# Segmented attention with batch norm: the start in another order, on other engines

## The chip, the cores and the metric

The kernel runs on one core of a Trainium2 chip. The metric is device time of one launch in microseconds (us), the median of several runs. The core has five engines with queues of their own: TensorE (PE, whose weight loads show as PEld), VectorE (DVE), ScalarE (ACT), GpSimd (POOL) and SyncE (SP). Each works through its own instructions in order and waits on semaphores for the others. SP, ACT and POOL also issue DMA transfers.

## The reference

16384 rows of 256 numbers belong to 8 segments by an id for each row (`bids`, here not sorted). Attention runs inside each segment, over at most 3072 positions.

```python
def _L0_rec_ref(feat, bids, Wq, Wk, Wv, Wt, gamma, beta):
    B = 8; LMAX = 3072; EPS = 1e-05; NEG = -1000000000.0
    N, d = feat.shape
    q = feat @ Wq
    k = feat @ Wk
    v = feat @ Wv
    starts = jnp.searchsorted(bids, jnp.arange(B, dtype=bids.dtype))
    pos = jnp.arange(N, dtype=bids.dtype) - starts[bids]
    def pad(x):
        return jnp.zeros((B, LMAX, x.shape[-1]), x.dtype).at[bids, pos].set(x)
    qp, kp, vp = (pad(q), pad(k), pad(v))
    mask = jnp.zeros((B, LMAX), bool).at[bids, pos].set(True)
    scores = jnp.einsum('bld,bmd->blm', qp, kp)
    scores = jnp.where(mask[:, None, :], scores, NEG)
    attn = jax.nn.softmax(scores, axis=-1)
    rp = jnp.einsum('blm,bmd->bld', attn, vp)
    r = rp[bids, pos]
    t = r @ Wt
    mu = t.mean(axis=0)
    var = t.var(axis=0)
    tn = (t - mu) / jnp.sqrt(var + EPS) * gamma + beta
    return feat + jax.nn.relu(tn)
```

Since the ids are not sorted, `starts` is the result of a binary search on unsorted data, and a row owns its slot only if its position falls inside the segment's window and no later row writes the same slot. So each segment has a few hundred owners, whose rows have to be found and gathered.

## The kernel before

All of it is written by hand in `fast_path`: the order of the calls of `pg` is the order of each engine's instructions, and `Program.op` works out which semaphores an instruction waits for from the places that it reads and writes (a strided write counts as the whole stretch between its first and last element). Only where a segment holds more than 4 tiles of 128 owners do the instructions for tiles 4 and 5 run (`present`, `given`: a branch on the tile count in `tiles_i`, which each engine loads into a register).

**The start (lines 1070 to 1425).** SP loads the ids (`b_i`), ACT the weights: `wv_sb`, `wt_sb`, and `w4`, which holds Wq three times and Wk once. SP also fills the rows' buffer `xs` of all 8 segments with zeros by eight DMAs (`zero_fill`), since a gather leaves a row alone where the index is out of range. DVE sets constants. Then comes the first list: segment 0's owners have a mask (`own0`); `scan` counts them along a partition into `lm`; `prefix` lets PE sum over the partitions (`tri`, `onesb`) and DVE derive where each partition's owners begin and end (`cbeg`, `cend`, `n_bc`, `tiles_i`); `list_tests` compares slot numbers with these (`ge`); `list_half` multiplies `lm` and `ge` on PE for three tiles, and its `finish` counts on DVE (`lr`, `junk`, `jc`) the index of each slot's row (`idx`) and lets POOL issue three gathers. Ten DVE instructions (`nwi` to `sm`) build a matrix for the binary search, which then runs in three steps of small products and comparisons (`less`, `hit1`, `hit2`, `stv`) to the starts `st_bc`. With them `owners(e)` finds the owners of any segment (6 operations and a scan), here of segment 1, whose list follows. PE then multiplies Wv and Wt (`wvT`, `wvt`), DVE sets six PSUM banks to 1.0, and segment 0's rows are transposed (`xT`, less the first tile's mean `negx`) and projected (`project`: q and k, from q and k copies of PSUM), give values (`values`, into `vs`, whose last column is ones for the softmax's sum) and scores with their exponentials (`scores`, `pa`). Banks for these come from `nb()`, which hands out two in turn.

**The segments (lines 1642 to 1700).** For segment e and tile u: `attend` multiplies exponentials and values, `attended` takes the reciprocal (`rdens`) on DVE and scales on ACT (`tk`), and in fixed steps u the next segment is transposed, projected and scored, the list of segment e + 2 is made, and column sums go on (`moments`, `acc`). Between them `slot(n)` takes n pieces of other work from a queue, by the table `plan_of`: first `everyone()` (a, b, c, d: positions and owners of all rows; f: the scans of segments 3 to 7 and of the losers; g: their prefix and the list tests of segment 3; h: how often each slot is read; g2: a table of output groups), then `tables()` and `one_hot()`.

**The end.** Rows outside the first six segments' slots are looked up again (`others`), the batch norm's sums are closed, and all groups of rows get their result added and stored.

## Time and profile before

| what | value |
|---|---|
| median of 3 runs | 338.47 us (337.35 to 339.0) |
| the profiled execution | 340.09 us |
| its span, first to last instruction | 337.7 us |
| PE, DVE, ACT, POOL busy in the span | 253.6, 231.1, 128.9, 130.9 us |
| mean granted TensorE clock | 0.882 |
| chain that ended last, by engine | PE 50%, DVE 19%, DMA 11%, issue 9%, POOL 6%, ACT 3% |
| first gather of rows, POOL | at 10.04 us |
| first product of exponentials and values, PE | at 49.76 us |

The profile comes from one execution and gives each instruction's start and duration, what its engine waited for, and the chain of work that ended last, followed back from the last instruction. A row of the timeline reads: start in us, duration in us, engine, line of the kernel (often that of a helper, so the tile's name says more), operation, what it writes and reads, its shape, how many were merged, and in brackets how long the engine had stood idle and who released it. PE's spans are modelled at their ends, so a busy PE need not be a fast one; the granted clock is shown apart.

### The profile page before, as it was taken

The numbers are of one execution on the slowest core, as the hardware profiler recorded it, in microseconds if no ns is written. First come the engines' busy times: TensorE is split into PE (matmuls) and PEld (weight loads), VectorE is DVE, ScalarE is ACT, GpSimd is POOL, SyncE is SP. The second block draws the span as 40 slices with busy tenths as digits, with TensorE's granted clock in tenths as the row PEclk, the third lists the DMA queues.
The fourth block names the chain that finished last, engine by engine and source line by source line (L and its number), as shares of the span: only waits on it lengthen the run. The fifth ranks groups of instructions, "written<-read, shape, count | busy, mean of one in ns | idle before, by whom it ended". The sixth has DMA issues, their size and how long they took to land.

```text
span 337.7 us, 4437 instructions
## 1 busy us (share of the span) xinstructions
PE 253.6 (75%) x1192; PEld 170.3 (50%) x1192; DVE 231.1 (68%) x714; ACT 128.9 (38%) x281; POOL 130.9 (39%) x143
## 2 busy tenths in 40 slices
PE   2227679689799989999999999939729889755100
PEld 1225347477487677777878778627513323112000
DVE  6677437966989898636665676737389999995400
ACT  0011343426756648644755664544402323121100
POOL 2617004306034015005721760741021146887775
PEclk9999698969899999999999999996957989895755
DMA  7992001213112103203030321592998899999982
GB/s 238 339 319 65 2 0 33 79 52 97 63 61 66 64 32 88 66 3 117 19 104 32 84 86 56 174 333 53 325 423 355 296 423 418 423 394 416 415 325 83
DMA packets 26186, 59.27 MB, mean 176 GB/s; under 512 B 5408, under 2 KB 18802, under 8 KB 22058
## 3 DMA queue, kind: packets, MB, share of 16 engines
q1 hardware_dynamic: 19242, 48.06, 38.6%
q0 software_dynamic: 5280, 10.18, 9.4%
q10 hardware_dynamic: 1632, 0.66, 0.7%
q8 instruction: 14, 0.23, 0.3%
q14 instruction: 18, 0.15, 0.2%
HBM read 26.80 MB, written 28.74 MB: 164 GB/s over the span
## 4 chain that ended last, share of the span: by engine, by line
PE 50%; DVE 19%; DMA 11%; issue 9%; POOL 6%; ACT 3%; POOLq 1%; DVEq 0%; ACTq 0%; SPq 0%
PE ps L807 47%; DMA out<-f 8%; POOL out L892 5%; PE ps L812 3%; DVE f L826 2%; DMA tl<-t_rows,ridl 2%; DVE tk L826 2%; ACT pa L817 1%; DVE acc L846 1%; DVE junk L833 1%; DVE w L826 1%; DVE k L823 1%; POOL xl L882 1%; DMA b_i<-in_r_bids 1%; DVE lm L855 1%
## 5 line engine op out<-in xcount | busy, mean ns | idle before, releaser
L882 POOL DMA_INDIRECT xs<-in_r_feat,idx x48 | 50.5, 1053 | 129.6 <-DVE idx L846 68.7
L807 PE MATMUL ps<-vs,pa 128*128 128x257 f32 x312 | 77.9, 403 | 6.5 <-ACT vs L822 4.6
L807 PEld LDWEIGHTS ps<-vs,pa 128*128 128x128 f32 x312 | 61.0, 201 | 18.5 <-ACT vs L822 5.0
L892 POOL DMA_INDIRECT out<-tk,idx x39 | 45.7, 1171 | 30.7 <-DVE f L826 14.6
L807 PE MATMUL ps<-wvt,xT 128*128 128x256 f32 x156 | 42.3, 424 | 1.7 <-DVE own L835 1.6
L817 ACT ACTIVATE tk<-ps,rdens 128x256 f32<-128x256 f32 x46 | 22.2, 482 | 55.7 <-DVE rdens L859 55.6
L807 PE MATMUL ps<-f,ident 128*128 128x512 f32 x56 | 35.0, 755 | 6.1 <-DMA f<-in_r_feat 6.1
L807 PEld LDWEIGHTS ps<-wvt,xT 128*128 128x128 f32 x156 | 32.2, 212 | 13.1 <-issue 3.2
L822 ACT COPY f<-ps 128x512 f32<-128x512 f32 x28 | 15.0, 589 | 54.8 <-PE ps L807 54.8
L807 PE MATMUL ps<-y,hot 48*128 48x256 bf16 x128 | 16.4, 312 | 14.7 <-DVE f L826 8.1
L817 ACT ACTIVATE pa<-ps,mask 128x512 f32<-128x512 f32 x39 | 23.9, 691 | 7.2 <-PE ps L807 7.2
L826 DVE TENSOR_TENSOR f<-f,ps 128x512 f32<-128x512 f32 x36 | 22.3, 681 | 4.2 <-DMA f<-in_r_feat 3.4
L826 DVE TENSOR_TENSOR tk<-tk,ss 128x1024 f32<-128x1024 f32 (+1 forms) x30 | 24.3, 848 | 0.3
L846 DVE SCALAR_TENSOR_TENSOR acc<-sq,reads_r,acc 128x256 f32<-128x256 f32 x45 | 21.6, 479 | 4.1 <-ACT sq L817 4.0
L823 DVE COPY k<-ps 32x128 f32<-32x128 f32 x40 | 11.8, 294 | 17.0 <-PE ps L807 16.2
L807 PEld LDWEIGHTS ps<-y,hot 48*128 48x128 bf16 x128 | 5.5, 101 | 35.0 <-issue 13.5
L846 DVE SCALAR_TENSOR_TENSOR acc<-tk,reads_r,acc 128x256 f32<-128x256 f32 x45 | 21.4, 476 | 1.2 <-ACT tk L817 0.6
L807 PEld LDWEIGHTS ps<-f,ident 128*128 128x128 f32 x56 | 11.2, 227 | 19.3 <-issue 10.7
L807 PE MATMUL ps<-q,k 32*128 32x512 f32 (+2 forms) x154 | 18.7, 478 | 2.9 <-ACT pa L817 2.9
L807 PE MATMUL ps<-xT,w 128*128 128x512 f32 (+1 forms) x60 | 20.1, 468 | 0.2 <-ACT xT L817 0.2
L807 PE MATMUL ps<-vs,pb 128*128 128x257 f32 x82 | 19.6, 388 | 0.0
L807 PEld LDWEIGHTS ps<-vs,pb 128*128 128x128 f32 x82 | 15.1, 190 | 6.5 <-issue 2.3
(249 smaller groups left out, 353.0 us busy)
## 6 DMA issues: line engine op xcount, KB each, us to landing
f<-in_r_feat SPq DMA_DIRECT2D x16, 1024.0 KB, 13.8
out<-f SPq DMA_DIRECT2D x16, 1024.0 KB, 11.7
xs<-zt SPq DMA_DIRECT2D x8, 768.0 KB, 10.8
t_rows<-tk SPq DMA_DIRECT2D x8, 512.0 KB, 2.9
t_rows<-tk SPq DMA_DIRECT2D x8, 256.0 KB, 2.3
eb<-edge_of SPq DMA_DIRECT2D x16, 96.0 KB, 2.4
xs<-in_r_feat,idx POOLq DMA_INDIRECT x48, 2.8
out<-tk,idx POOLq DMA_INDIRECT x39, 6.6
```

The lines of the kernel that those rows point to most:

```text
L807: "PE", lambda e: e.matmul(out, lhsT, rhs, start=start, stop=stop, skip_group_check=True),
L812: return self.op("PE", lambda e: e.transpose(out, in_, ident), [in_, ident], [out])
L817: "ACT", lambda e: e.activation(out, in_, func, bias=bias, scale=scale), [in_, *more], [out]
L822: return self.op("ACT", lambda e: e.copy(out, in_), [in_], [out])
L823: return self.op(eng, lambda e: e.tensor_copy(out, in_), [in_], [out])
L826: return self.op(eng, lambda e: e.tensor_tensor(out, a, b, op), [a, b], [out])
L833: lambda e: e.tensor_scalar(out, a, s1, s2, op0, op1, accum_out=accum)
L846: else e.scalar_tensor_tensor(out, a, s, b, op0, op1),
L855: "DVE", lambda e: e.tensor_tensor_scan(out, a, b, 0.0, ALU.mult, ALU.add), [a, b], [out]
L882: lambda e: e.indirect_dma_start(out=out, out_offset=None, in_=table, in_offset=bass.IndirectOffsetOnAxis(ap=ind, axis=0), bounds_check=n ...
L892: lambda e: e.indirect_dma_start(out=table, out_offset=bass.IndirectOffsetOnAxis(ap=ind, axis=0), in_=src, in_offset=None, bounds_check=n ...
```

## The change

The order of the start is written anew, and some work changes its engine.

- Constants: the ten instructions `nwi` to `sm` stand ahead of the ids' cast. `zt` and several constants are set by POOL. Later, DVE's memsets of `vs`'s ones, `acc`, `xl`, `tl`, `ridl` and `ecat` go to POOL too, behind the gathers of segment 1.
- Loads: Wq and Wk are loaded once each, on SP's queue behind the ids; ACT makes the two further copies of Wq.
- Zeros and blanks: ACT writes the zeros of `xs` for segments 0 to 2 and the ones of the six banks. The DMA fills of segments 3 to 7 stay on SP's queue, behind the small loads.
- First list: `prefix` returns three parts (`first`, `then`, `last_`) that are called apart, `list_tests` has two parts, and the search's products and comparisons stand between those of the list.
- Value weights: PE turns and multiplies them between the search's steps.
- Segment 0: each tile is transposed on its own (`turned`), in two banks, and moved in two halves.
- Segment 3 gets `owners` of its own as one piece of work (`third`), after b; the scans and the prefix of `everyone` begin at segment 4, and `steps` says in which steps a piece is taken.

On ACT, this stood from the start to the first activation that writes `xT` before:

```order
L877 DMA wv_sb<-in_L_rec_Wv 128x2x256
L877 DMA wt_sb<-in_L_rec_Wt 128x2x256
L877 DMA w_68<-in_L_rec_Wq 128x2x32
L877 DMA w_68<-in_L_rec_Wq 128x2x32 [waits of_ACT_2]
L877 DMA w_68<-in_L_rec_Wq 128x2x32 [waits of_ACT_3]
L877 DMA w_68<-in_L_rec_Wk 128x2x32 [waits of_ACT_4]
L694 BRANCH_PREFETCH_HINT
L688 TENSOR_LOAD tiles_i [waits at_DVE]
L688 ISA x2
L822 ACT_TABLE_LOAD
L822 COPY wvT<-ps 128x256 [waits at_PE] x2
L822 COPY wvt<-ps 128x256 [waits at_PE] x2
```

And this stands there now (`w_68` is `w4`, `of_SP_2` the landing of Wk):

```order
L822 ACT_TABLE_LOAD
L822 COPY ps<-ones 128x512 [waits at_DVE]
L822 COPY ps<-ones 128x512
L822 COPY xs<-zt 128x1536 [waits at_POOL]
L822 COPY ps<-ones 128x512 x4
L822 COPY w_68<-w_68 128x2x32 [waits of_SP_2]
L822 COPY w_68<-w_68 128x2x32 [waits at_ACT]
L822 COPY xs<-zt 128x1536
L822 COPY wvT<-ps 128x256 [waits at_PE] x2
L822 COPY wvt<-ps 128x256 [waits at_PE]
L822 COPY xs<-zt 128x1536
L822 COPY wvt<-ps 128x256 [waits at_PE]
```

The blanks, zeros and copies of Wq are new there, ahead of the value weights' copies; the register load moved behind `xT`.

POOL's queue from its constants on (each DMA row is one gather of 128 rows; the twelve are segment 0's and segment 1's) is changed thus:

```order
 L694 BRANCH_PREFETCH_HINT
+L865 MEMSET reads_r 128x48
+L865 MEMSET eps_t 128x1
+L865 MEMSET ones_n 128x128
+L865 MEMSET rdens 128x48
+L865 MEMSET graw 128x64
 L882 DMA xs<-in_r_feat,idx 128x256 x12
+L865 MEMSET vs_61 128x6
+L865 MEMSET vs_66 128x6
+L865 MEMSET acc 128x512
+L865 MEMSET xl 128x768
+L865 MEMSET tl 128x768
```

The memsets of `vs_61` (`vs[0]`, segment 0's values) stand behind all twelve gathers; ACT's first copy into it waits for POOL.

On PE, in segment 0's steps (the first piece is behind tile 3's product, the second stood ahead of segment 1's second values), the prefix of the fourth list moves up and gets one column:

```order
@@ -99,4 +104,6 @@
 L772 UNCONDITIONAL_BRANCH
 L807 MATMUL ps<-vs_61,pa_60 128x257
+L807 MATMUL ps<-lm,tri 128x1
+L807 MATMUL ps<-lm,onesb 128x1
 L772 COMPARE_AND_BRANCH
 L807 MATMUL ps<-xT,w_68 128x128 x2
@@ -125,6 +132,4 @@
 L807 MATMUL ps<-vs_61,pb 128x257 x6
 L772 UNCONDITIONAL_BRANCH
-L807 MATMUL ps<-lm,tri 128x6
-L807 MATMUL ps<-lm,onesb 128x6
 L807 MATMUL ps<-wvt,xT 128x256 x4
```

The prefix of segments 4 to 7 and of the losers, now five columns, is taken in segment 1. The diff, cut to its core:

```diff
+    pg.dma("SP", w4[:, :, 0:DQ], wq.rearrange("(h p) m -> p h m", p=P))
+    pg.dma("SP", w4[:, :, 3 * DQ : 4 * DQ], wk.rearrange("(h p) m -> p h m", p=P))
...
-    zero_fill(0)
+    blank(slice(4, 6))
+    zero_rows(0)
+    blank(slice(0, 4))
+    for g in (1, 2):
+        pg.copy("ACT", w4[:, :, g * DQ : (g + 1) * DQ], w4[:, :, 0:DQ])
+    zero_rows(1)
...
+    sA, sB = ps_o
+    pg.mm(sA[:, 0:NB], sm[:], less[:])
+    pg.mm(sB[:, 256:257], sm[:], ones[:, 0:1])
+    first()
+    list_tests(0, FT, 0)
+    h0 = list_half(0, 0, nb())
+    then()
...
+    pg.mm(sB[:, 0:NB], b_f[:], hit1[:])
+    h1 = list_half(0, 1, nb())
+    list_tests(0, FT, 1)
+    h0()
...
+    pg.mm(sA[:, 0:NB], sm[:], less[:])
+    wv_turned(0)
+    wv_turned(1)
+    h1()
...
+    wv_wt(0)
+    pg.mm(sB[:, 0:NB], ones[:], stv[:])
...
+    zero_rows(2)
...
+    bx = [bank[0], bank[1]]
+    def turned(t):
+        for h in range(DH):
+            pg.tr(bx[h][:, t * P : (t + 1) * P], xs[:, t, h * P : (h + 1) * P], ident[:])
+    last_()
+    owners(1)
+    turned(0)
+    for h in range(DH):
+        pg.red(xsum[:, h : h + 1], bx[h][:, 0:P])
+    wv_wt(1)
+    turned(1)
+    first, then, last_ = prefix(1, 2)
...
+    first()
+    list_tests(1, FT, 0)
+    turned(2)
...
+        into_xT(h, 0, QB, bx[h][:, 0:QB])
+    h0, h1 = list_half(1, 0, ps_s[2]), list_half(1, 1, ps_s[3])
+    turned(3)
...
+        into_xT(h, QB, QA, bx[h][:, QB:QA])
+    h0()
     for eng in ("PE", "ACT", "DVE"):
         pg.register(eng, 0, tiles_i[0:1, 0:1], 2)
...
     project(0, 0)
     xt_rest(0)
+    h1()
+    last_()
+    for i in range(2):
+        pg.set("POOL", vs[i][:, :, D : D + 1], 1.0)
+    pg.set("POOL", acc[:], 0.0)
...
+    for e in range(3, NB):
+        pg.dma("SP", xs[:, e * FT : (e + 1) * FT, :], zt[:].unsqueeze(1).to_broadcast([P, FT, D]))
     values(0, 0)
...
-            for e in range(3, NB):
+            for e in range(4, NB):
                 pg.scan(lm[:, e, 0:J], ones[:], o3[:, e, :])
...
-    plan_of = {(0, u): n for u, n in enumerate((0, 1, 2, 1, 1, 1))}
-    for e in range(1, NB - 1):
-        for u in range(FT):
-            plan_of[(e, u)] = 1 if e > 3 else int(u in ((0, 2, 4) if e == 1 else (0, 2, 3, 5)))
-    work.extend(everyone())
+    steps = {0: (1, 2, 3, 4, 5), 1: (0, 1, 2, 4, 5), 2: (0, 2, 3, 5), 3: (0, 1, 2, 3, 5)}
+    def third():
+        owners(3)
+        first, then, last_ = prefix(3, 4, ps_s[3])
+        first()
+        then()
+        last_()
+        list_tests(3, FT)
+    todo = everyone()
+    work.extend([*todo[0:2], third, *todo[2:]])
```

More of the change, by code (lines that the diff above doesn't have):

```diff
@@ L1097, in fast_path @@
-    pg.set("DVE", eps_t[:], EPS)
-    pg.set("DVE", ones_n[:], 1.0 / N)
-    pg.set("DVE", rdens[:], 1.0)
+    pg.ts(nwi[:, 0:1], pci[:], -1, ALU.mult)
+    pg.tt(nwi[:, 0:1], nwi[:, 0:1], pci[:], ALU.bitwise_and)
+    pg.copy("DVE", wfl[:, 0:1], nwi[:, 0:1])
+    pg.tt(wfl[:, 1:2], pcol[:], wfl[:, 0:1], ALU.subtract)
+    pg.tt(wfl[:, 0:1], pcol[:], wfl[:, 0:1], ALU.add)
+    pg.ts(sa[:], irow[:], pcol[:], ALU.is_ge)
+    pg.stt(sm[:], irow[:], wfl[:, 0:1], sa[:], ALU.is_lt, ALU.mult)
+    pg.ts(sc_[:], irow[:], wfl[:, 1:2], ALU.is_ge)
@@ L1107, in fast_path @@
+    blank(slice(4, 6))
[4 more added lines that the diff above has]
+    zero_rows(1)
     pg.dma("SP", bs_i[0 : P - PS, :], bids2[PS:P, :])
     pg.dma("SP", br_i[PS:P, :], bids2[0 : P - PS, :])
-    for e in range(1, NB):
-        zero_fill(e)
-    pg.set("DVE", graw[:], 0.0)
+    pg.set("POOL", reads_r[:], 0.0)
+    pg.set("POOL", eps_t[:], EPS)
+    pg.set("POOL", ones_n[:], 1.0 / N)
+    pg.set("POOL", rdens[:], 1.0)
@@ L1112, in fast_path @@
+    pg.set("POOL", graw[:], 0.0)
     for i in range(4):
@@ new lines, in fast_path, with wv_turned, wv_wt @@
+    pg.ts(hit1[:], sA[:, 0:NB], popc[:, 0:1], ALU.is_equal)
+    pg.mm(sB[:, 0:NB], b_f[:], hit1[:])
+    h1 = list_half(0, 1, nb())
+    list_tests(0, FT, 1)
+    h0()
+    pg.tt(less[:], sB[:, 0:NB], ecol[:], ALU.is_lt)
+    pg.ts(ident[:], irow[:], pcol[:], ALU.is_equal)
+    def wv_turned(m):
+        b = bank[m]
+        for h in range(DH):
+            pg.tr(b[:, h * P : (h + 1) * P], wv_sb[:, h, m * P : (m + 1) * P], ident[:])
+        pg.copy("ACT", wvT[:, m, :], b[:, 0:D])
+    def wv_wt(h):
+        b = bank[2 + h]
+        for m in range(DH):
+            pg.mm(b[:, 0:D], wvT[:, m, h * P : (h + 1) * P], wt_sb[:, m, :], start=(m == 0), stop=(m == 1))
+        pg.copy("ACT", wvt[:, h, :], b[:, 0:D])
@@ L1358, in fast_path @@
     pg.tt(stv[:], stv[:], lowp[:], ALU.add)
-    ps = nb()
-    pg.mm(ps[:, 0:NB], ones[:], stv[:])
-    pg.copy("DVE", st_bc[:], ps[:, 0:NB])
+    wv_wt(0)
+    pg.mm(sB[:, 0:NB], ones[:], stv[:])
+    pg.copy("DVE", bs_f[:], bs_i[:])
+    pg.tt(same[:], bs_f[:], b_f[:], ALU.is_equal)
+    pg.copy("DVE", st_bc[:], sB[:, 0:NB])
     pg.ts(st_lo[:], st_bc[:], -float(LMAX), ALU.add)
     pg.ts(st_hi[:], st_bc[:], float(LMAX), ALU.add)
-    pg.copy("DVE", bs_f[:], bs_i[:])
-    pg.tt(same[:], bs_f[:], b_f[:], ALU.is_equal)
+    zero_rows(2)
     def owners(e):
@@ L1379, in fast_path @@
+    h0()
     for eng in ("PE", "ACT", "DVE"):
         pg.register(eng, 0, tiles_i[0:1, 0:1], 2)
-    for m in range(DH):
-        b = nb()
-        for h in range(DH):
-            pg.tr(b[:, h * P : (h + 1) * P], wv_sb[:, h, m * P : (m + 1) * P], ident[:])
-        pg.copy("ACT", wvT[:, m, :], b[:, 0:D])
-    for h in range(DH):
-        b = nb()
-        for m in range(DH):
-            pg.mm(b[:, 0:D], wvT[:, m, h * P : (h + 1) * P], wt_sb[:, m, :], start=(m == 0), stop=(m == 1))
-        pg.copy("ACT", wvt[:, h, :], b[:, 0:D])
@@ L1393, in fast_path @@
-    pg.tr32(gb[:].rearrange("p s i -> p (s i)"), graw[:].rearrange("p s i -> p (s i)"))
-    for b in bank[0:6]:
-        pg.set("DVE", b[:], 1.0)
-    for i in range(2):
-        pg.set("DVE", vs[i][:, :, D : D + 1], 1.0)
-    pg.set("DVE", acc[:], 0.0)
-    pg.ts(rc[:], n_bc[:, 0:1], float(P), ALU.min, 1.0, ALU.max)
-    pg.recip(rc[:], rc[:])
-    bx = [nb(), nb()]
-    for t in range(4):
-        for h in range(DH):
-            pg.tr(bx[h][:, t * P : (t + 1) * P], xs[:, t, h * P : (h + 1) * P], ident[:])
@@ L1425, in fast_path @@
     owners(2)
-    list_tests(2, FT)
+    first, then, last_ = prefix(2, 3)
+    first()
+    list_tests(2, FT, 0)
+    then()
+    list_tests(2, FT, 1)
+    last_()
+    pg.tr32(gb[:].rearrange("p s i -> p (s i)"), graw[:].rearrange("p s i -> p (s i)"))
     work = []
@@ L1462, in g @@
         def g():
[L1463 to L1464 removed]
+            for go in prefix(4, NL, ps_s[3]):
+                go()
         def g2():
```

145 lines of the change are left out of this document (62 added, 83 removed).

## The prediction

> **What bounds the kernel now.** I first cut the span into stages with the table of busy time by window (PE, PEld, DVE, ACT and POOL busy with counts, granted clock, DMA share, GB/s), then read the chain that ended last.
>
> ```profile
> 0.00:49.40 49.40, 23.77 (x95) 15.93 (x95) 29.03 (x152) 8.97 (x16) 14.40 (x39) 0.93 0.54 164
> 49.40:75.60 26.20, 22.20 (x103) 16.76 (x104) 20.77 (x83) 9.01 (x18) 6.98 (x7) 0.80 0.17 53
> 75.60:97.70 22.10, 20.03 (x97) 14.89 (x96) 17.40 (x69) 14.33 (x31) 6.17 (x7) 0.92 0.24 74
> ...
> 125.00:207.00 82.00, 82.00 (x465) 64.71 (x463) 51.92 (x171) 47.63 (x112) 32.98 (x31) 1.00 0.22 64
> ...
> 131.81 23.29 PE ps L807 x120
> ```
>
> From 125 to 207 us PE is busy all of the time, and the chain runs through it in long unbroken pieces (23.29 us at 131.81): whatever arrives earlier at 125 leaves earlier. What follows (repeated rows, statistics, output) hangs on that stage by data, so I pass a gain at 125 through whole. In the first 49.4 us no engine is the limit: PE is busy 23.8, DVE 29.0, ACT 9.0. This is one serial chain, and the change is mostly about it.
>
> **The change part by part.** I follow four stations: the cast of the segment ids (b_f), the end of the scan of segment 1's owners, the end P of segment 0's first projection, and A, the first product of weights and values.
>
> ```profile
> 0.88 0.27 DVE L865 MEMSET zt<- 128x256 f32 x1 [0.88 <-PEq L1919]
> ...
> 3.68 0.23 DVE L823 CAST b_f<-b_i 128x128 f32<-128x128 int32 x1 [0.80 <-DMA b_i<-in_r_bids]
> ...
> 8.85 0.16 DVE L846 SCALAR_TENSOR_TENSOR idx<-ps,jc 128x3 int32<-128x3 f32 x1
> 8.93 0.14 DVE L835 TENSOR_SCALAR nwi<-pci 128x1 int32<-128x1 int32 x1
> ...
> 10.04 1.19 POOL L882 DMA_INDIRECT xs<-in_r_feat,idx  x1 [7.67 <-DVE sa L835]
> ...
> 10.99 0.29 DVE L826 TENSOR_TENSOR sm<-sm,sa 128x128 f32<-128x128 f32 x1
> ```
>
> Station 1. DVE waits 0.80 for the ids, so it is ready at 2.88. The ten rows nwi to sm (8.93 to 11.28, 2.35 us) now stand ahead of the cast; out go zt (0.27), ident and five smaller memsets, by that row some 0.9 (at least 0.27, at most the 2.0 since 0.88). So b_f starts at 2.88 - 0.9 + 2.35 = 4.3: **0.6 later**. The first index takes 5.17 after b_f now; four small operations leave its way (0.3), so it comes at 9.2 and its gather, 1.2 behind it as here, at 10.3 instead of 10.04. The second half of the list no longer has the ten rows in front.
>
> ```profile
> 17.71 0.17 DVE L823 COPY st_bc<-ps 128x8 f32<-128x8 f32 x1 [0.69 <-PE ps L807]
> ...
> 18.53 0.22 DVE L835 TENSOR_SCALAR own<-b_f 128x128 f32<-128x128 f32 x1
> ...
> 20.48 0.43 DVE L855 TENSOR_TENSOR_SCAN lm<-ones,own 128x128 bf16<-128x128 f32 x1
> ...
> 22.04 1.28 ACT L822 ACT_TABLE_LOAD   x1 [22.04 <-DVE armf L835]
> ...
> 27.35 3.62 PE L807 MATMUL ps<-wt_sb,wvT 128*128 128x256 f32 x8
> ...
> 27.59 0.37 ACT L822 COPY wvT<-ps 128x256 f32<-128x256 f32 x1 [1.15 <-PE ps L812]
> ...
> 43.57 0.59 ACT L822 COPY vs<-ps 128x512 f32<-128x512 f32 x1 [3.68 <-PE ps L807]
> ```
>
> Station 2. The search now runs beside the list, but its last product (stv) stands on PE behind four transposes and half of the value weights. These start when ident is written, at about 10; four transposes (one of the eight passes of 3.62 takes 0.45 and is twice as wide, so 0.35 a piece, 1.4), the last copy of 0.37 and 1.3 of passes behind it end at 13.1; stv, for which DVE waits 0.69 today, is copied at 13.7 instead of 17.71. The owners follow 0.8 later and take 2.4 (18.53 to 20.91): the scan ends at 16.8, **4.1 earlier**. ACT, idle until 22.04 today, hides the blanks and zeros: 1.8 + 1.28 + six copies of 0.59 + two zero fills. No row shows a 128x1536 copy; between the step from 256 to 512 elements (0.22, so 1.45) and three copies of 0.59 (1.77) I take 1.45. ACT is free at 9.9, and its first wvT copy is due at 10.7: hidden, by 0.8.
>
> ```profile
> xs<-in_r_feat,idx POOLq DMA_INDIRECT x6, 7.2
> ...
> xs<-in_r_feat,idx POOLq DMA_INDIRECT x48, 2.8
> ...
> 22.45 1.72 PE L807 MATMUL ps<-lm,ge 128*128 128x131 bf16 x12 [1.28 <-DVE ge L835]
> ...
> 33.01 0.49 DVE L851 TENSOR_REDUCE xsum<-ps 128x1 f32<-128x128 f32 x2 [0.35 <-PE ps L812]
> 33.54 0.60 DVE L835 TENSOR_SCALAR negx<-xsum,rc 128x2 f32<-128x2 f32 x1
> ...
> 34.17 1.26 ACT L817 ACTIVATE xT<-ps,negx 128x512 f32<-128x512 f32 x2 [2.79 <-DVE negx L835]
> ...
> 35.49 2.99 PE L807 MATMUL ps<-xT,w 128*128 128x512 f32 x4
> ...
> 38.52 1.22 DVE L823 COPY k<-ps 32x128 f32<-32x128 f32 x4 [2.74 <-PE ps L807]
> ```
>
> Station 3. Today 14.6 us lie between the scan's end and the projection: the second list, the value weights, six blanks on DVE, eight transposes, the sums. Now the gathered rows themselves are on the path. Beside the zero fills (window 9 to 18 us) a gather lands 7.2 us after its issue, over the whole run 2.8. The five fills left on the SP queue follow Wq, Wk, the shifted ids and eight small loads there, so they begin near 9 and meet these gathers again. With 2.8, the scan sets the pace: sums and negx to 18.3, tile 2 turned by 18.8, first xT half and the 12 list products (1.5 of the 1.72, which holds a wait) to 20.9, tile 3 turned and second xT half (1.3) to 22.3, projection 2.99: P = 25.3. With 7.2, tile 0 lands at 17.5, negx is ready at 19.9, tile 2 lands at 20.1, and the same steps end at P = 27.0. I take 26.3, **12.2 earlier** than 38.5 (ends 13.2 and 11.5).
>
> ```profile
> 32.59 1.00 POOL L882 DMA_INDIRECT xs<-in_r_feat,idx  x1 [0.30 <-issue]
> ...
> 44.53 1.99 PE L807 MATMUL ps<-wvt,xT 128*128 128x256 f32 x8
> 44.62 2.42 ACT L817 ACTIVATE pa<-ps,mask 128x512 f32<-128x512 f32 x4 [0.47 <-PE ps L807]
> ...
> 49.76 3.52 PE L807 MATMUL ps<-vs,pa 128*128 128x257 f32 x8
> ```
>
> Station 4 has a **new wait**. The ones column of vs is now set by POOL, and stands there behind the gathers of segment 1's second list half. That half is finished on DVE behind the k copies. So from P: k copies 1.25, list half 1.6, to the gather 1.0, three gathers at 1.3 make 3.9, two small memsets 0.2: the vs copy can start at P + 7.95, against P + 5.07 now (43.57 - 38.5). Behind it on ACT stand the four pa activations (2.42), and values(0, 1) on PE waits for the bank it empties. From the end of pa to A are 2.7 today, 0.35 less with fewer operations ahead of ge: A = P + 13.35, if PE stays at full clock; if values(0, 1) runs at the slow 3.50 of segment 0's first values rather than 1.99, the second vs copy is last, and A = P + 14.4. Against P + 11.26 that is 2.1 to 3.1 lost; I take 2.6.
>
> ```profile
> 50.00:52.00 2.00, 2.00 (x6) 1.56 (x6) 1.81 (x5) 0.00 (x0) 0.00 (x0) 0.50 0.02 4
> ...
> 40.03 3.50 PE L807 MATMUL ps<-wvt,xT 128*128 128x256 f32 x8 [1.55 <-DVE own L835]
> ```
>
> The granted clock falls to 0.50 after short idle stretches (50 to 52 us). [...]
>
> So A moves by 12.2 - 2.6 = **9.6 earlier** (49.76 to 40.15).
>
> ```profile
> 57.91 3.64 PE L807 MATMUL ps<-vs,pa 128*128 128x257 f32 x16
> ...
> 59.42 1.23 DVE L826 TENSOR_TENSOR w<-m,st_bc 128x1024 f32<-128x1024 f32 x1
> ...
> 66.44 1.69 DVE L855 TENSOR_TENSOR_SCAN lm<-ones,o 128x128 bf16<-128x128 f32 x5
> ...
> 68.50 0.19 PE L807 MATMUL ps<-lm,tri 128*128 128x6 bf16 x1 [3.95 <-DVE rdens L859]
> ...
> 68.58 3.76 PE L807 MATMUL ps<-wvt,xT 128*128 128x256 f32 x8
> ...
> 82.33 0.15 DVE L835 TENSOR_SCALAR g<-irow 1x16 f32<-1x16 f32 x1
> ...
> 85.05 0.20 DVE L835 TENSOR_SCALAR over<-n_bc 128x8 f32<-128x8 f32 x2
> ```
>
> The fourth list. In segment 0, PE waits 3.95 for DVE's work on all segments and then runs 3.76 where 1.99 was enough. Now only owners(3) (2.4) stands between w (ends 60.65) and the prefix, and PE gets there when its products with pa end at 61.55: with a reciprocal between, it waits about 1.8. But the list tests (1.2) and a small prefix (0.9) delay the next reciprocal, so pa and vs of segment 1 follow late; by rows the next A-like product comes 2.0 earlier (bounds 0.5, and 3.95 + 1.77 - 1.8 = 3.9): **2.2 earlier**. In segment 1 DVE pays it: o and five scans (2.9) and the prefix (0.95) come in, where 4.7 of 22.1 us were idle. The table of groups (g to over, 82.33 to 85.25, 2.9) moves from the third step to the fifth and lets go of the pa activations that PE waits for, which saves up to 0.7 there; at the segment's end DVE is then 2 late. Between -0.7 and +3.9 (all on the path) I take **0.9 later**, nearer to the end where DVE's idle time covers it. DVE's memsets given to POOL lie beside PE work and count nothing.
>
> The sum: 9.6 + 2.2 - 0.9 = 10.9. The profiled execution took 340.09 us (its span is 337.7, the 2.4 around it stay), which gives 329.2. It lay 1.6 over the median of 338.47; taken from that, **327.6**.
>
> **The rivals.**
> - The POOL wait is not felt (k copies or gathers sooner than I think): the 2.6 come back, 325.0. For it: POOL's spans are rough; against it: the chain from P is made of durations that hardly vary. 0.15.
> - The work doesn't lie beside the loads: ACT stands in order on the copies of Wq, which wait for Wk, and SP issues Wk only when Wq has landed.
>
> ```profile
> w<-in_L_rec_Wq ACTq DMA_DIRECT2D x3, 32.0 KB, 6.3
> ```
>
>   At 6.3 each, Wk lands at 13.8, ACT's next zeros end at 15.7 and wvT starts 5 late; less what the 7.2 us gathers hide, P is 4 later: 331.6. Against it: those 6.3 were beside the fills, which now start after it. 0.12.
> - Segments 1 and 2 give back all that DVE gains in work (3.9 instead of 0.9): 330.6. For it: PE already stands idle for 2.1 of the 22.1 us there, and the table operations that follow in segment 2 are as heavy; against it: DVE's 4.7 idle. 0.13.
> - Slower: the fills starve the first gathers. P follows tile 0's landing by 9.5; A then equals today's, plus the 1.3 of the later terms, at P = 37.2, that is a landing 17.4 us after issue. At 20 us the time is 341.1. Against it: 7.2 is the measured middle under seven fills, and now five run. 0.03.
>
> **How the numbers follow.** My forecast has 0.57, the rivals 0.15, 0.12, 0.13 and 0.03. The range takes in the first three: below, P = 25.3 without the POOL wait and with 3.9 in segment 0 would be 322.3; above, the ACT rival with a late segment 1 is 333.5. So 322 to 333.5. Only a loss of over 1.7 us is slower by 0.5% (about what a measurement of this kernel can tell from no change): faster 0.94, same 0.03, slower 0.03.
>
> **What would show it.** In the changed profile: b_f near 4.3; the first gather near 10.3 and landings above 5 us; the scan of segment 1 ending near 16.8; project near 23; ACT's first vs copy waiting for POOL, 8 us behind the projection; the first product with pa near 40; a prefix wait under 2 us in segment 0; PE without a gap over segments 3 to 5. It is wrong if the vs copy does not wait, if ACT stands still before wvT, or if segments 1 and 2 take over 52 us together.

## The result and the profile after

| | before | after |
|---|---|---|
| median, first comparison | 338.55 us (4 runs) | 328.57 us (4 runs) |
| ratio | | 0.970 (0.967 to 0.974) |
| median, second comparison, on chip B below | 336.95 us (17 runs) | 329.12 us (6 runs) |
| ratio | | 0.981 (0.973 to 0.988) |
| profiled execution, its span | 340.09, 337.7 us | 327.83, 325.4 us |
| mean granted TensorE clock | 0.882 | 0.894 |

The change is faster by 2 to 3%: 10.0 us in the first comparison and 7.8 in the second, where the forecast had 10.9. Single runs of one kernel spread over 2 to 7 us, so a difference of one or two microseconds is read from the profiles below, not from the times; each of these shows one execution. The ratios compare fast runs only, and of the profiled executions only that of `fills_late` (331.83 us) was a slow one.

First the table of busy time by window of the kernel after, for the stages that the prediction cut out of the one before: PE, PEld, DVE, ACT and POOL busy with counts, granted clock, DMA share, GB/s.

```profile
0.00:39.15 39.15, 20.95 (x100) 15.26 (x101) 24.80 (x137) 17.21 (x29) 17.53 (x52) 0.94 0.47 146
39.15:60.57 21.42, 19.34 (x99) 14.58 (x97) 17.06 (x76) 8.91 (x18) 6.08 (x6) 0.94 0.20 58
60.57:85.72 25.15, 20.95 (x100) 14.12 (x97) 21.13 (x87) 14.31 (x31) 6.17 (x6) 0.93 0.22 70
113.40:197.80 84.40, 83.55 (x471) 65.57 (x469) 54.08 (x179) 48.04 (x113) 33.76 (x31) 1.00 0.20 62
```

Almost the whole gain lies ahead of 39 us: ACT's busy time there rose from 9.0 to 17.2, POOL's from 14.4 to 17.5, and DVE's fell by 4. In the third row, segment 1, 4.2 of 25 us of PE are idle, more than before. The stage from 113 to 198 is still PE, now with 0.9 us idle.

The timeline of the kernel after gives the stations (start, duration, engine, line, operation, and in brackets the idle time before it and what ended that).

```profile
1.68 0.76 POOL L870 IOTA it<- 128x768 f16 x1
1.77 0.71 DVE L835 TENSOR_SCALAR nwi<-pci 128x1 int32<-128x1 int32 x1
...
4.61 0.22 DVE L823 CAST b_f<-b_i 128x128 f32<-128x128 int32 x1
...
10.60 1.20 POOL L882 DMA_INDIRECT xs<-in_r_feat,idx  x1 [7.56 <-DVE junk L833]
...
13.74 0.17 DVE L823 COPY st_bc<-ps 128x8 f32<-128x8 f32 x1 [0.96 <-PE ps L807]
16.43 0.43 DVE L855 TENSOR_TENSOR_SCAN lm<-ones,own 128x128 bf16<-128x128 f32 x1
17.83 0.69 PE L812 MATMUL ps<-ident,xs 128*128 128x128 f32 x2 [4.13 <-DMA xs<-in_r_feat,idx]
...
21.66 1.14 PE L807 MATMUL ps<-lm,ge 128*128 128x131 bf16 x12
...
23.47 1.98 PE L807 MATMUL ps<-xT,w 128*128 128x512 f32 x4 [0.46 <-ACT xT L817]
...
33.02 0.59 ACT L822 COPY vs<-ps 128x512 f32<-128x512 f32 x1 [6.16 <-POOL vs L865]
33.66 2.71 PE L807 MATMUL ps<-wvt,xT 128*128 128x256 f32 x8 [3.62 <-ACT vs L822]
39.15 3.18 PE L807 MATMUL ps<-vs,pa 128*128 128x257 f32 x8
...
52.02 0.18 PE L807 MATMUL ps<-lm,tri 128*128 128x1 bf16 x1 [1.53 <-DVE lm L855]
...
65.24 0.18 PE L807 MATMUL ps<-lm,tri 128*128 128x5 bf16 x1 [1.89 <-DVE idx L846]
65.90 3.42 PE L807 MATMUL ps<-xT,w 128*128 128x512 f32 x4
84.40 1.14 PE L807 MATMUL ps<-vs,pa 128*128 128x257 f32 x4 [1.92 <-ACT sq L817]
```

The new wait is there: ACT stands 6.16 us for POOL's two tiny memsets of vs, and PE 3.62 behind it. So is a wait for data that the kernel before hid, 4.13 us for tile 0 of the gathered rows. The wait of 3.95 for DVE in segment 0 is 1.53 now; in segment 1 there are two new ones, and between them a projection at a granted clock of 0.50 (66 to 68 us), 3.42 against 1.88 before.

What became of it, by the start of the eight transposes in the first step of each segment (they turn the next segment's rows), which both kernels have:

| transposes in segment | before | after | earlier by |
|---|---|---|---|
| 0 | 53.58 | 42.52 | 11.06 |
| 1 | 75.46 | 60.57 | 14.89 |
| 2 | 97.52 | 85.72 | 11.80 |
| 3 | 124.90 | 113.40 | 11.50 |
| 4 | 154.93 | 144.55 | 10.38 |
| 6 | 208.19 | 197.82 | 10.37 |
| end of the span | 337.7 | 325.4 | 12.3 |

From a row to the next is what a segment takes: segment 0 took 21.88 us and takes 18.05, segment 1 took 22.06 and takes 25.15, so that 3.1 are given back there. Below, "segment 1's transposes" are those of its row.

### The profile page after: what moved, and what is told of

Read it like the earlier page. It is cut to its first block, busy times and chain, and to the rows that moved or that the text cites. A ratio compares the mean times of both kernels' runs of the same rounds, so it can differ in the third digit from the quotient of the medians.

```text
span 325.4 us, 4462 instructions
## 1 busy us (share of the span) xinstructions
PE 249.6 (77%) x1194; PEld 166.4 (51%) x1194; DVE 227.3 (70%) x709; ACT 136.8 (42%) x294; POOL 133.8 (41%) x156
## 5 line engine op out<-in xcount | busy, mean ns | idle before, releaser
L817 ACT ACTIVATE tk<-ps,rdens 128x256 f32<-128x256 f32 x46 | 22.2, 483 | 61.5 <-DVE rdens L859 61.3
L807 PE MATMUL ps<-wvt,xT 128*128 128x256 f32 x156 | 37.9, 390 | 5.7 <-ACT vs L822 3.6
L807 PEld LDWEIGHTS ps<-wvt,xT 128*128 128x128 f32 x156 | 29.1, 191 | 15.7 <-ACT vs L822 4.6
L807 PEld LDWEIGHTS ps<-y,hot 48*128 48x128 bf16 x128 | 5.6, 101 | 35.3 <-DVE f L826 13.7
L807 PE MATMUL ps<-xT,w 128*128 128x512 f32 (+1 forms) x60 | 20.8, 479 | 0.6 <-ACT xT L817 0.5
```

Of the source, the lines that this page charges most:

```text
L807: "PE", lambda e: e.matmul(out, lhsT, rhs, start=start, stop=stop, skip_group_check=True),
L817: "ACT", lambda e: e.activation(out, in_, func, bias=bias, scale=scale), [in_, *more], [out]
```

## The experiments

Each is an edit of the kernel after. They ran on three chips, on each of them beside the kernel before: `fills_late`, `ones_early`, `owners_step_later` and `no_fourth_alone` on chip A (before: 337.56 us), `again`, `search_late`, `weights_late` and `ones_early_busy` on chip B (336.95), the last four on chip C (347.7).

**1. What sets the start of the projection.** Three runs each take one part of the start back or apart.

`fills_late`: the zero fills wait for segment 0's last gather.

```diff
     for e in range(3, NB):
-        pg.dma("SP", xs[:, e * FT : (e + 1) * FT, :], zt[:].unsqueeze(1).to_broadcast([P, FT, D]))
+        pg.dma("SP", xs[:, e * FT : (e + 1) * FT, :], zt[:].unsqueeze(1).to_broadcast([P, FT, D]), [rows[FT - 1]])
```

> The changed kernel with one edit: the five zero fills left on SP's queue wait for the last gather of segment 0, so that none runs beside its six gathers. Theory (the fills make the first gathers land 7.2 us after issue, and tile 0 sets the start of the projection): tile 0 lands about 3 us after its issue at 10.6, PE no longer waits 4.1 us before its transposes, segment 0's projection starts 1.0 to 1.5 us earlier (22.0 to 22.5 instead of 23.47), where the owner scan of segment 1 (16.86) is the next limit; ratio 0.966. Rival 1 (the slow landing is the gathers' own): tile 0 still lands near 17.8 and nothing moves, 0.970. Rival 2: the fills, now at 22 to 37 us, delay segment 1's gathers and the gain is given back before segment 1's transposes, 0.970 or above.

Measured: 328.46 us, ratio 0.972 (0.967 to 0.977). The timeline of this run:

```profile
13.64 0.69 PE L812 MATMUL ps<-ident,xs 128*128 128x128 f32 x2
17.19 0.66 PE L812 MATMUL ps<-ident,xs 128*128 128x128 f32 x2 [1.16 <-DVE xsum L851]
...
21.35 3.67 PE L807 MATMUL ps<-xT,w 128*128 128x512 f32 x4 [0.35 <-ACT xT L817]
```

The fills did make the landing slow: tile 0 is transposed 3.0 us after its gather's issue at 10.60, as soon as PE is free, and the next limit is DVE with the owner scan and the sums. The projection starts 2.1 us earlier, more than expected. It then takes 3.67 instead of 1.98, so that its end moves by 0.4 only, and later stretches of this execution ran slow too: the granted clock is 0.78 from 42 to 60 us, where the kernel after has 1.00. Four of the six executions took 326.35 to 329.55 us, so these stretches say little of the edit. The gain at the station is shown; that it reaches the end is not.

`search_late`: the search for the starts stands behind the first list again.

```diff
-    pg.ts(less[:], ecol[:], b_f[:, 0:1], ALU.is_gt)
-    pg.mm(sA[:, 0:NB], sm[:], less[:])
...
     wv_turned(1)
     h1()
+    pg.ts(less[:], ecol[:], b_f[:, 0:1], ALU.is_gt)
+    pg.mm(sA[:, 0:NB], sm[:], less[:])
...
```

> The changed kernel with one part undone: the search for the segments' starts stands behind the whole of the first list again, not inside it. Theory of the prediction for landings of 7.2 us (tile 0 at 17.8 sets the pace, the owner scan of segment 1 has 3 us of slack behind it): the scan ends 2 to 2.5 us later than 16.9, but the projection starts within 0.7 us of 23.5, ratio 0.970 to 0.973. Rival (the scan sets the pace): the projection moves with it, 2 to 2.5 us, ratio 0.977.

`weights_late`: the products of the value weights stand ahead of segment 0's projection again.

```diff
-    wv_turned(0)
-    wv_turned(1)
     h1()
...
     h0()
+    wv_turned(0)
+    wv_turned(1)
+    wv_wt(0)
+    wv_wt(1)
```

> The changed kernel with one part undone: the products of the value weights stand right ahead of segment 0's projection, as before, instead of while the rows load. Theory (PE's 4.0 us of products and 1.1 us of transposes were hidden in the wait for tile 0, only half of the second product stood beside it): the projection starts 3 to 4 us later than 23.5, ratio 0.979 to 0.982. Rival (PE is not on the path here, the lists on DVE are): projection within 1 us of 23.5, ratio 0.970.

`again`: the kernel after unchanged, on the same chip as these two.

> The changed kernel itself, unchanged, beside the others on one chip. All theories: ratio 0.966 to 0.974. What tells them apart is its profile: where the same instructions up to segment 1 run at other clocks than in the first profile of it (first projection 1.98, first product with pa 3.18, the second values of segment 1 1.99), the granted clock there differs from execution to execution, and stations of two profiles can be compared only from one event to the next.

Measured: `again` 329.12 us, ratio 0.981 (0.973 to 0.988), `search_late` 330.55, 0.985 (0.976 to 0.993), `weights_late` 333.6, 0.993 (0.989 to 0.997). The timelines of `search_late` and `weights_late`:

```profile
19.50 0.43 DVE L855 TENSOR_TENSOR_SCAN lm<-ones,own 128x128 bf16<-128x128 f32 x1
...
21.98 1.66 PE L807 MATMUL ps<-lm,ge 128*128 128x131 bf16 x12
...
24.41 3.00 PE L807 MATMUL ps<-xT,w 128*128 128x512 f32 x4 [0.35 <-ACT xT L817]
...
62.53 1.04 PE L812 MATMUL ps<-ident,xs 128*128 128x128 f32 x8
```

```profile
27.21 1.88 PE L807 MATMUL ps<-xT,w 128*128 128x512 f32 x4
...
47.38 1.04 PE L812 MATMUL ps<-ident,xs 128*128 128x128 f32 x8
```

Without the search inside the list the scan is 3.1 us later, and the projection starts 0.9 later. The weights are another thing: taken out of the wait, they make the projection 3.7 us later, segment 0's transposes 4.9, and the time 4.5, as expected. The ratios of all three runs lie higher than expected, and are compared with that of `again`.

What was expected of `again` failed in its ratio, but its profile has the same granted clocks as the first one (0.81 from 24 to 42 us, 1.00 from 42 to 60), and its stations agree within 0.05 us up to segment 2's transposes (23.45, 42.50, 60.54, 85.72). Both profiles are of the fastest execution of their set. Other profiles differ at the same place without an edit there. From 21 us on PE does the same work at one of two rates: the twelve list products ahead of the projection take 1.14 us in the kernel after, `again` and `no_fourth_alone`, and 1.65 or 1.66 in `search_late` and in `ones_early`, `owners_step_later` and `owners_after_rows` below. The start of `ones_early` has only two memsets more, and the edits of the last two come after 60 us. The projection starts at 24.13 to 24.23 in these three and takes 3.21, 2.72 and 3.19. The granted clock reads 1.00 from 0 to 24 us in all of them, so that the rates differ by the clock is not shown; only the durations differ.

So `search_late` is to be compared with a profile of the same rate. That of `owners_after_rows`:

```profile
24.22 3.19 PE L807 MATMUL ps<-xT,w 128*128 128x512 f32 x4 [0.35 <-ACT xT L817]
...
62.53 1.04 PE L812 MATMUL ps<-ident,xs 128*128 128x128 f32 x8
```

Here the search is worth 0.2 us at the projection's start and nothing at its end (27.41 in both) or at segment 1's transposes: what it gains waits for tile 0.

No run took back the other parts of the start (the blanks and zeros on ACT, the loads of Wq and Wk, the transposes tile by tile), so how the rest of the 13.0 us at the projection's end (38.48 before, 25.45 after) divides among them stays open.

**2. The wait for POOL, and the clock.** `ones_early` sets the ones ahead of the gathers.

```diff
     pg.set("POOL", graw[:], 0.0)
+    for i in range(2):
+        pg.set("POOL", vs[i][:, :, D : D + 1], 1.0)
...
-    for i in range(2):
-        pg.set("POOL", vs[i][:, :, D : D + 1], 1.0)
     pg.set("POOL", acc[:], 0.0)
```

> The changed kernel with one edit: POOL sets the ones columns of vs (two memsets of 0.16 us together) with its early memsets, ahead of every gather, instead of behind segment 1's last three gathers. Theory (the new POOL wait is on the path): ACT's first vs copy no longer waits for POOL and starts when the first values are done, near 29.0 us instead of 33.0; values(0, 1) follow at 30 at full clock, the first product with pa starts near 35.1 instead of 39.15, and nearly all of it, 3 to 4 us, arrives at the end: ratio to the kernel before 0.958 to 0.962 (0.970 for the changed kernel). Rival (segment 0 is bound by DVE, whose work on all segments then comes late instead): the product with pa is early, but segment 1's transposes stay within 1 us of 60.6 and the ratio stays at 0.967 to 0.970.

Measured: 327.52 us, ratio 0.969 (0.964 to 0.975). Its timeline:

```profile
24.13 3.21 PE L807 MATMUL ps<-xT,w 128*128 128x512 f32 x4 [0.35 <-ACT xT L817]
...
30.91 0.59 ACT L822 COPY vs<-ps 128x512 f32<-128x512 f32 x1 [2.15 <-PE ps L807]
...
35.69 1.16 DVE L835 TENSOR_SCALAR ge<-it,cbeg 128x768 bf16<-128x768 f16 x1
35.86 0.75 POOL L865 MEMSET tl<- 128x768 f32 x1
36.77 0.76 DVE L835 TENSOR_SCALAR ge<-it,cend 128x768 bf16<-128x768 f16 x1
38.10 3.04 PE L807 MATMUL ps<-vs,pa 128*128 128x257 f32 x8
```

Counted from the projection's end (27.34 here, 25.45 in the kernel after), the vs copy comes after 3.6 instead of 7.6 us and the first product with pa after 10.8 instead of 13.7: the wait cost 2.9. But the projection itself ended 1.9 later: it started 0.7 later and took 1.2 longer, at the lower rate described above. So the product comes only 1.05 earlier on the scale, segment 2's transposes 1.3, and at the end the spans are 325.2 and 325.4. Beside profiles with the same rate at the start, the gain stays: segment 1's transposes come at 59.38, against 62.53 in `search_late` and `owners_after_rows`, and the span is 2.4 shorter than that of `search_late` (327.6). The ratio is the rival's, then, but not for the rival's reason: segment 0 is not bound by DVE. One cost shows that nobody expected: the two ge operations take 1.16 and 0.76 instead of 0.41 each, with POOL's memsets of 768 and 512 elements (0.75 and 0.73) now beside them.

`ones_early_busy` adds products that only keep PE running.

```diff
+    def turn_over(n, ps):
+        for _ in range(n):
+            pg.mm(ps[:, 300:428], ident[:], ident[:])
...
+    turn_over(14, sB)
     turned(0)
...
     project(0, 0)
     xt_rest(0)
+    turn_over(6, sB)
...
     first, then, last_ = prefix(2, 3)
+    turn_over(8, sB)
...
+        turn_over(8, ps_s[3])
         first, then, last_ = prefix(3, 4, ps_s[3])
```

> ones_early with filling products on PE: 14, 6, 8 and 8 products of the identity with itself, into columns that nothing reads, stand in front of the waits for tile 0 (4.1), for DVE behind the projection (1.6), for segment 2's list tests (1.7) and for segment 3's prefix (1.5). Theory (what is left of PE's slow stretches before 66 us comes from the clock, which falls when PE idles): granted clock 0.97 or more from 24 to 60 us (0.91 and 1.00 in ones_early's two windows), the first projection takes 1.98 and the first product with pa 1.96 instead of 3.2 and 3.04, segment 1's transposes start near 57 instead of 59.4, ratio 0.960 to 0.964. Rival 1 (the products themselves hold the path, or the clock falls at the same places all the same): segment 1's transposes at 59 to 61, ratio 0.968 to 0.972.

Measured: 324.62 us (322.3 to 326.6) beside 329.12 for the kernel after on the same chip, whose runs are all at 327.9 or above; ratio to the kernel before 0.966 (0.959 to 0.973). Windows and timeline of it:

```profile
24.00:42.00 18.00, 16.32 (x99) 12.41 (x98) 12.67 (x60) 7.04 (x13) 11.56 (x29) 1.00 0.13 39
42.00:60.00 18.00, 16.25 (x95) 12.86 (x93) 16.11 (x63) 7.70 (x17) 7.58 (x8) 1.00 0.24 76
```

```profile
22.97 1.98 PE L807 MATMUL ps<-xT,w 128*128 128x512 f32 x4 [0.64 <-ACT xT L817]
37.63 1.04 PE L812 MATMUL ps<-ident,xs 128*128 128x128 f32 x8
...
55.94 1.04 PE L812 MATMUL ps<-ident,xs 128*128 128x128 f32 x8
...
81.00 1.04 PE L812 MATMUL ps<-ident,xs 128*128 128x128 f32 x8
```

The granted clock is 1.00 in both windows (0.81 and 1.00 in the kernel after). From 24 to 42 us it is 1.00 in all three profiles with these first three groups of products, and 0.71 to 0.91 in the nine of the kernel after and its edits without any. Segment 0's transposes are 4.9 us earlier than in the kernel after, 3.7 earlier than with the early ones alone. In segment 3 the lead is still 4.7 (108.69 against 113.40); the span gains 3.1. So this kernel beats the kernel after, beside which it ran. `ones_early` ran on another chip, and the intervals of the two ratios overlap. Part of the lead goes near 210 us. There PE waits for a vs copy that stands on ACT behind the square of repeated rows (ecat), and this for their gather. PE's wait before, after (with ACT's row) and in `ones_early_busy`:

```profile
228.25 9.31 PE L807 MATMUL ps<-vs,pa 128*128 128x257 f32 x28 [4.58 <-ACT vs L822]
```

```profile
216.00 0.42 ACT L817 ACTIVATE ecat<-tl 128x256 f32<-128x256 f32 x1 [3.36 <-DMA tl<-t_rows,ridl]
...
216.94 9.09 PE L807 MATMUL ps<-vs,pa 128*128 128x257 f32 x28 [3.56 <-ACT vs L822]
```

```profile
213.36 8.88 PE L807 MATMUL ps<-vs,pa 128*128 128x257 f32 x28 [4.69 <-ACT vs L822]
```

PE arrives 4.7 us earlier than in the kernel after and waits 1.1 longer.

**3. The fourth list.** `no_fourth_alone` takes that part back.

```diff
-            for e in range(4, NB):
+            for e in range(3, NB):
                 pg.scan(lm[:, e, 0:J], ones[:], o3[:, e, :])
...
-            for go in prefix(4, NL, ps_s[3]):
+            for go in prefix(3, NL, ps_s[3]):
                 go()
+            list_tests(3, FT)
...
-    work.extend([*todo[0:2], third, *todo[2:]])
+    work.extend(everyone())
```

> The changed kernel without its fourth list on its own: the owner scans of segment 3 stand again with those of the others, the prefix runs over segments 3 to 8 in one piece, and the steps are those of the kernel before. It computes the same. Theory of the prediction: the fourth list alone is worth 2.2 in segment 0 less 0.9 in segment 1, so without it 1.3 us more: ratio 0.974, segment 1's transposes 2.2 later (62.8). What the trace after suggests instead: 3.75 gained in segment 0 and all of it given back in segments 1 and 3 (segment 1's transposes near 64.3, segment 2's within 0.7 us of 85.7), ratio 0.968 to 0.971.

Measured: 327.56 us, ratio 0.973 (0.968 to 0.977). Its timeline:

```profile
42.55 1.04 PE L812 MATMUL ps<-ident,xs 128*128 128x128 f32 x8
...
63.49 1.04 PE L812 MATMUL ps<-ident,xs 128*128 128x128 f32 x8
...
83.98 1.04 PE L812 MATMUL ps<-ident,xs 128*128 128x128 f32 x8
```

Up to segment 0's transposes it is the kernel after to 0.03 us. Then segment 0 takes 20.9 instead of 18.05 us and segment 1 20.5 instead of 25.15: the fourth list alone wins 2.9 and gives back 4.7. Segment 3, where the edit also sets back the order of steps, takes 30.03 as in the kernel before, against 31.15 in the kernel after. So the kernel without it is 1.7 ahead at segment 2's transposes, 3.2 at segment 4's (141.33 against 144.55) and 2.6 in the span. Neither expectation had this: the prediction's had it 1.3 behind, the other level. Both are profiles of the fastest execution of their set; the ratios, 0.973 against 0.970 and 0.981, do not tell the kernels apart.

`busy_no_fourth_alone` makes the same comparison with the filling products.

> ones_early_busy without the fourth list on its own (all owner scans and the prefix over segments 3 to 8 in segment 0 again, the steps of the kernel before; three of the four groups of filling products). It computes the same. If the fourth list alone is worth its 3 us in segment 0 and gives them back in segment 1 (no_fourth_alone: 20.9 and 20.5 us in segments 0 and 1 against 18.05 and 25.15), segment 2's transposes come at 79 to 81 as in ones_early_busy (81.0) or earlier, ratio 0.960 to 0.966. By the prediction's net of 1.3 in its favour they come at 82.3 and the ratio is 0.970.

Measured on chip C: 335.22 us, ratio 0.963 (0.958 to 0.968). Segments 0 and 1 take 22.4 and 22.5 us (18.3 and 25.1 in `ones_early_busy`), and segment 2's transposes come at 83.11 instead of 81.00, later than both expectations; at segment 4's the distance is 0.6 (140.45 and 139.85). Here its segment 0 lost by the clock, which was 0.81 from 42 to 60 us, and the fourth group of filling products, which stood ahead of this list's prefix, is missing. So this pair does not settle what the fourth list is worth; its size is under what the times can tell.

Two runs move the work that segment 1 took over. `owners_step_later` puts it one step later, `owners_after_rows` to the end of the first step.

```diff
-    steps = {0: (1, 2, 3, 4, 5), 1: (0, 1, 2, 4, 5), 2: (0, 2, 3, 5), 3: (0, 1, 2, 3, 5)}
+    steps = {0: (1, 2, 3, 4, 5), 1: (1, 2, 3, 4, 5), 2: (0, 2, 3, 5), 3: (0, 1, 2, 3, 5)}
```

> The changed kernel with one edit: in segment 1 the steps are (1, 2, 3, 4, 5) instead of (0, 1, 2, 4, 5), so the owners' work on all segments (o and five scans, 3.0 us of DVE) stands behind segment 3's list instead of before its second half, and the prefix behind it one step later. Theory (segment 1 gave back 3 us because this work holds the reciprocal and the second list half, and PE waits 1.89 at the prefix and then runs the projection at half clock, 3.42 instead of 1.9): the 1.89 wait goes, the projection takes under 2, segment 2's transposes start 1.5 to 3 us earlier than 85.7, ratio 0.961 to 0.966. Rival (DVE's sum of work in segment 1 is the limit, wherever it stands): another wait of the same size takes its place, segment 2's transposes stay within 0.7 us of 85.7, ratio 0.969 to 0.972.

```diff
-    steps = {0: (1, 2, 3, 4, 5), 1: (0, 1, 2, 4, 5), 2: (0, 2, 3, 5), 3: (0, 1, 2, 3, 5)}
+    steps = {0: (1, 2, 3, 4, 5), 1: (2, 3, 4, 5), 2: (0, 2, 3, 5), 3: (0, 1, 2, 3, 5)}
...
                 xt_main(n, 1)
+                if e == 1:
+                    slot()
```

> The changed kernel with one edit in segment 1: the owners' work on all segments (o and five scans, 3.0 us of DVE) stands behind segment 3's list and segment 2's transposes of the first step instead of before the reciprocal of that step, and the prefix two steps later; the other steps stay. Theory (that block gave back the 3 us: it holds a reciprocal, with it ACT's rows and xT and the second list half, so that PE waits 1.9 at the prefix and then runs the projection at half clock): from segment 1's transposes to segment 2's are 22 to 23 us instead of 25.15 in both profiles of the changed kernel, ratio lower than that kernel's by 0.006 to 0.010. Rival (DVE's sum in segment 1 is the limit, so the next DVE wait grows by as much): 24.5 us or more, ratio unchanged.

Measured: `owners_step_later` 331.9 us, ratio 0.983 (0.978 to 0.989), the opposite of what was expected; `owners_after_rows` 341.57 on chip C, 0.984 (0.978 to 0.990), not lower either. Window and timeline of `owners_step_later`:

```profile
42.00:60.00 18.00, 16.12 (x64) 11.41 (x63) 13.70 (x56) 6.67 (x13) 7.43 (x6) 0.78 0.17 52
...
45.13 1.57 PE L812 MATMUL ps<-ident,xs 128*128 128x128 f32 x8
...
66.58 1.04 PE L812 MATMUL ps<-ident,xs 128*128 128x128 f32 x8
...
69.42 1.88 PE L807 MATMUL ps<-xT,w 128*128 128x512 f32 x4
...
89.95 1.04 PE L812 MATMUL ps<-ident,xs 128*128 128x128 f32 x8
```

In segment 1 the edit does what was expected of it: the wait of 1.89 before the projection is gone, the projection takes 1.88 again, and the segment 23.4 us instead of 25.15. What is left are other waits, 1.3 and 1.9 for ACT's squares at the prefix and at the segment's end and 1.0 before scores. But this execution lost 6.0 us before the edited place: 2.6 up to segment 0's transposes, and 3.4 in segment 0, 21.45 instead of 18.05. There the granted clock from 42 to 60 us is 0.78 instead of 1.00, behind the same wait of 1.53. All six of its runs lie at 329.5 or above; whether the edit makes the slow clock likelier was not settled.

In `owners_after_rows` segment 1 takes 24.5 us (62.53 to 87.01): the rival's number, and not the 22 to 23 expected. The wait and the slow projection are gone here too (65.36, 1.88), but at the segment's end, behind the wait of 1.93, the last products take 1.99 instead of 1.14 and the transposes 1.58 instead of 1.04; the granted clock is 0.94 from 85 to 113 us, where the kernel after has 1.00. With the same edit and the filling products, below, the clock is 1.00 from 60 to 113 us and the segment takes 23.4.

**4. Put together.** `best_ones_busy_after_rows` is `ones_early_busy` with the edit of `owners_after_rows`; `best_with_fills_late` adds the late fills, with 4 filling products in the first place.

> ones_early_busy (ones columns early, filling products) together with the edit of owners_after_rows. If the gains are apart in place they add up: segment 1's transposes near 56, segment 2's near 78.5, and 1 to 1.5 of the 2 to 2.5 us saved in segment 1 reach the end, since the wait for the repeated rows near 210 us (4.5 in ones_early_busy) grows as PE comes earlier: 322 to 323.5, ratio about 0.962. Rival: segment 1 is bound by DVE and the ratio stays that of ones_early_busy, 0.966.

> best_ones_busy_after_rows and besides the five zero fills behind segment 0's last gather (as in fills_late), with 4 filling products in the first place instead of 14, since the wait there is gone. Theory (fills_late gained 2.1 us up to the projection's start, 21.35, and lost it again to a slow clock): with the clock kept up the projection ends near 23.3 and segment 1's transposes start 1.5 us earlier than without the edit, ratio lower by 0.002 to 0.005. Rival (the fills at 21 to 37 us now delay segment 1's gathers): no gain.

Measured on chip C: 335.44 us, ratio 0.965 (0.960 to 0.970), and 333.96, ratio 0.962 (0.956 to 0.968). In place the first does nearly what was expected (segment 1's transposes at 55.99, segment 2's at 79.36, 1.7 us saved in segment 1), but the ratio cannot tell it from `ones_early_busy` at 0.966. In the second the projection starts 1.7 us earlier, and in its profile the gain is gone 10 us later:

```profile
21.36 1.98 PE L807 MATMUL ps<-xT,w 128*128 128x512 f32 x4 [0.46 <-ACT xT L817]
...
32.38 0.16 PE L807 MATMUL ps<-lm,tri 128*128 128x1 bf16 x1 [2.40 <-ACT vs L822]
...
32.43 3.46 PE L807 MATMUL ps<-ident 128*128 128x128 f32 x16
```

ACT's second vs copy waits 1.27 us, which its row puts down to "remote", not to any engine. PE stands 2.4, and the eight filling products take 3.46 instead of 2.03 in the first of the two kernels; the granted clock from 24 to 42 us is 0.91, there 1.00. Segment 0's transposes come at 38.22 against 37.68 there, segment 1's at 56.35 against 55.99. That the fills, which now run at this time, cause it is argued from their place, not shown. The profiled execution is also the longest of the six (338.05 us, four took 333.3 to 334.03), so the others may lack this stall. The medians' difference of 1.5 us is within what single runs spread.

## Why the prediction was right, step by step

The time on record was 327.6; the medians are 328.57 and 329.12, inside its range. The forecast case is also the one that happened in the start: the POOL wait is felt, and ACT is not held by Wk. But one of the signs that the prediction named for being wrong did come: segments 1 and 2 take 52.83 us together (60.57 to 113.40), over its 52. They give back 3.4, near the 3.9 of the third rival, and the sum held because more had been gained before.

- **Station 1.** b_f at 4.61 instead of the 4.3 predicted, the first gather at 10.60 instead of 10.3. The missing 0.3 lies in a stall that the sum did not have: beside POOL's iota of 768 elements nwi takes 0.71 (0.14 before), and with it the cast comes 2.84 after nwi's start instead of 2.35; nwi itself started 0.2 earlier than the sum has it.
- **Station 2.** st_bc at 13.74 (13.7 predicted), the scan ends at 16.86 (16.8). ACT's row fill takes 1.47 (1.45 estimated). `search_late` beside `owners_after_rows` shows that these 3.1 us are worth 0.2 at the projection's start and nothing at its end: the prediction's case of slow landings held, and in that case the scan is not the limit.
- **Station 3.** Tile 0 lands at 17.83, 7.2 us after issue, as in the slow end of the bracket, and `fills_late` shows its cause. P is 25.45 and not 26.3. The projection's start was right (23.47, against 23.3 by the middle of the bracket and 24.0 by its slow end); that it then takes 1.98 instead of the 2.99 carried over is luck, since profiles with an unedited start have 2.72 and 3.19 too.
- **Station 4.** The vs copy starts at P + 7.57 (7.95 predicted), and the first product with pa at P + 13.7, between the two ends that were given (13.35 and 14.4). The loss by the wait was taken as 2.6; `ones_early` measures 2.9. A moved by 10.6 instead of 9.6, and the difference is the projection's 1.98 against 2.99. Of the clock the prediction had two cases at the new wait, the values behind it at 1.99 or at 3.50, and so 0.5 either way of the loss that it took. They took 2.71, between the two. But over all the places with an idle PE that bound was too small: the same projection took 1.98 to 3.21 in different runs, and segment 0 18.05 or 21.45 us with the same 1.53 us wait in it, at a granted clock of 1.00 and of 0.78 from 42 to 60 us. So with the same wait the clock was up in one run and down in another; what decides it was not shown.
- **The fourth list, segment 0.** 3.8 earlier (14.89 less 11.06) instead of 2.2, at the bound of 3.9. Not all of it is the list's: `no_fourth_alone` puts 2.9 to it, and the other 0.9 (21.88 against 20.94 without the list) no run took apart. The prefix wait was 1.53 (1.8 predicted).
- **Segment 1.** This is the term that was mis-sized: 3.1 later instead of 0.9, inside its bounds. "Nearer to the end where DVE's idle time covers it" was the wrong choice. DVE's idle time here does not cover work that is put in front of a reciprocal: the whole block of 3.0 us holds the first step's reciprocal, ACT's rows and xT, and the second list half, and PE then meets a wait of 1.89 and a slow projection. `owners_step_later` takes 1.8 of it back by moving the block alone. With 2.9 won and 4.7 given back, beyond the bound of 3.9 (`no_fourth_alone`), this part of the change loses 1.7 us by segment 2 in the profiles and earns nothing that the times show, against the net 1.3 on record.
- **The rest.** Segment 3 gave back 1.1, where 31.15 us stand against 30.03. The prediction had nothing there; it belongs to the fourth list's part of the change with its new steps, since `no_fourth_alone` takes 30.03 again. From 198 us on 1.9 came back. Of it 1.0 is the wait for the repeated rows, 3.56 instead of 4.58; the prediction passed the gain at 125 through whole, while this wait takes or gives a microsecond by when its gather's own chain is ready. The errors of 1 to 2 us had both signs, and so the sum came out within 1.5 in the time (328.57, 329.12) and in the span (12.3 earlier, 10.9 predicted). So close a sum is in part luck. In the second comparison the gain is 7.8, 3.1 less than predicted.
- **The rivals.** ACT held by Wq and Wk: refuted, Wq lands in 3.0 us beside no fills, and the 1.39 that ACT stands before wvT it waits for PE. The wait for POOL not felt: refuted. Starving fills: a landing of 7.2, not 17.4.

## What to carry to other kernels

Before an engine is given small jobs, look at who stands behind them in its queue: two memsets of 0.16 us together behind three gathers cost 2.9 us, as much as many a good idea brings. Idle time of an engine did not make the added work free here: it held the engine's next urgent small operation, and moving it behind that gave part of the loss back. When PE waits in several places, compare kernels from one event to the next within a profile and note the granted clock of each stretch, since one stage took 3.4 us more where it read 0.78 instead of 1.00; filling the waits with idle products was worth more here than shortening one of them (segment 0's transposes 3.7 us earlier by the products, 1.2 by the early ones).
